# The last pair of a GNN kernel by batch element, its scores added on VectorE

## The chip, the cores and the metric

The kernel runs on one core of one Trainium2 chip. The metric is device time in microseconds of one execution. A core has TensorE (PE in the profile; its weight loads are PEld), VectorE (DVE), ScalarE (ACT), GpSimd (POOL) and SyncE (SP), each with its own instruction queue, and 16 DMA engines that all queues share.

## The reference

Two layers on 64 graphs of 256 nodes with 256 features; an adjacency matrix of zeros and ones for each graph. Each layer is `x = x + layer(relu(layernorm(x)))`. The first is a gated graph network of three steps, the second a graph attention with four heads:

```python
# layer 0, three steps
m = einsum('bnd,de->bne', h, weight[i])
aggr = einsum('bst,bsd->btd', A, m)
h = gru_cell(aggr, h, w_ih, w_hh, b_ih, b_hh)
# layer 1
h = (x @ W.T + b).reshape(B, N, H, C)
l_src, l_dst = einsum(h, a_src), einsum(h, a_dst)          # one score per node and head
logits = leaky_relu(l_src[:, :, None, :] + l_dst[:, None, :, :], 0.2)
logits = where(adj[..., None] == 1, logits, NEG_INF)
out = einsum('bijh,bjhc->bihc', softmax(logits, axis=2), h)
```

## The kernel before

Two batch elements make a pair; there are 32 pairs, numbered 0 to 31. All work is entered into a plan by tick and is emitted in that order (`at`, L307; L777 to 780). Pair p starts at tick 18p, so three pairs are under way at a time: while one runs its last step (its ticks 24 to 29), the one before it prepares its attention and the one before that computes its outputs. A tick has three phases, STEP, READY and REST, in this order, and within a phase the later pair comes first. Each engine carries out its instructions in the order in which they were emitted. Below, ticks of pair 31 are counted from its own start, and those of pair 30 are converted to that count (its own minus 18).

A step (`Step`, L365) has six ticks. It works on both elements together and shares products between them, so that its blocks of eight matmuls (`block`, L289; `pd`, `pc`, `pe`, `pn` are their PSUM banks) belong to both. `new_n` ends with a subtraction on GpSimd (L487), and `update` (L499) gives the new state of one element with two VectorE instructions. After the last step (`back`, L544) the state is transposed and added to x.

The attention of a pair then goes as follows; the ticks in brackets are those of pair 31 in the kernel before.

- `plan_norm` and `plan_relu_T` (32 to 36): statistics and normal form of the four row blocks of x on VectorE, one power on GpSimd, eight transposes and a Relu on ScalarE into `hT_b`.
- `bar` (35): VectorE makes the mask `noedge` from the integers `adj`, loaded by SP at tick 22.
- `values` (37, 38): products with the weights, `val`, and the scores of both kinds.
- `score_rows` (37, 38 for the two elements of the last pair): the scores are transposed, copied into `flat` (one buffer), and written to DRAM by SP. SP then reads the target scores back on all partitions, as `drow`.
- `linked` and `barred_in` (36 to 41): the mask is transposed (`plink`, `link`; one `link` buffer), and ScalarE fills the logits `zz` with it. `zz` has four buffers, two for each pair.
- `add_rows` (41, 42): GpSimd issues a DMA that adds the source scores from DRAM into `zz`.
- `maxima` (43 to 50) and `leaky` (48 to 55): the largest target score of each node among its neighbours, on VectorE; leaky relu, on ScalarE.
- `shift` and `shift_rows` (47 and 51 for the two elements): the row maxima, written to DRAM as `topT`. In the last pair SP reads them back as `mrow`, and VectorE adds them to `zz` in `exps`; in the other pairs a second adding DMA does it (pair 30: ticks 38 and 39).
- `exps` (60 to 63) and `output` (62 to 65): exponentials on ScalarE, 16 matmuls `po` for each of the four row blocks, division on VectorE, addition to x on GpSimd. At tick 66 SP writes out the pair.

Pair 30's maxima stand at ticks 25 to 32, its leaky relus at 30 to 37, its exponentials at 42 to 45, its outputs at 44 to 47. Pair 29's outputs stand at 26 to 29.

The lines that hold the order:

```python
STEP, READY, REST = range(3)
plan.setdefault(tick, ([], [], []))[phase].append((-p, fn))
...
for tick in sorted(plan):
    for phase in plan[tick]:
        for _, fn in sorted(phase, key=lambda y: y[0]):
            fn()
```

Of the kernel before, what the change touches and what calls it, by code (L numbers as in the profile page):

```python
# [9 lines left out]
F32 = mybir.dt.float32  # L10
# [16 lines left out]
def gated_gnn_then_gat_kernel(  # L27
# [282 lines left out]
    def plan_norm(src, name, p, ticks):  # L310

        v = {}

        def stats(r0):
            def fn():
                if not v:
                    v["st"] = small.tile([P, R, 6], F32, tag="st", name=f"st_{name}")
                    v["mv"] = small.tile([P, R, 2], F32, tag="mv", name=f"mv_{name}")
                for r in (r0, r0 + 1):
                    nc.vector.bn_stats(v["st"][:, r, :], src()[:, r, :])  # L320
                    nc.vector.bn_aggr(v["mv"][:, r, :], v["st"][:, r, :])
            return fn

        def deviation():
            rstd = v["rstd"] = small.tile([P, R], F32, tag="rstd", name=f"rstd_{name}")
            nc.vector.tensor_scalar_add(rstd, v["mv"][:, :, 1], EPS)
            nc.gpsimd.tensor_tensor(rstd, rstd, mhalf, ALU.pow)

        def result():
            xn = v["xn"] = buf("xn", [P, R, D], f"xn_{name}")  # L330
            for r in range(R):
                nc.vector.tensor_scalar(
                    xn[:, r, :], src()[:, r, :], v["mv"][:, r, 0:1], v["rstd"][:, r : r + 1],
                    op0=ALU.subtract, op1=ALU.mult,
                )

        for t, fn in zip(ticks, (stats(0), stats(2), deviation, result)):
            at(t, READY, p, fn)
        return v

    def plan_relu_T(v, tag, name, p, ticks):

        w = {}

        def fn(k):
            def go():
                if not w:
                    w["hT"] = buf(tag, [P, KD, T], f"hT_{name}")
                pt = bank(f"pt_{name}_{k}")
                for r in range(R):  # L350
                    nc.tensor.transpose(pt[:, ts(r, P)], v["xn"][:, r, ts(k, P)], ident)  # L351
                nc.scalar.activation(w["hT"][:, k, :], pt, AF.Relu)
            return go

        for k, t in enumerate(ticks):
            at(t, REST, p, fn(k))
        return w

    def by_c(y):
        return y.rearrange("q (c n) -> q c n", c=KD)  # L360

    def of(y, i):
        return y[:, :, ts(i, N)]

    class Step:  # L365


        def __init__(self, n_, l, hT):
            self.n_, self.l, self.hT = n_, l, hT

        def own(self, tag, shape):
            y = buf(tag, shape, f"{tag}_{self.n_}")
# [107 lines left out]
        def new_n(self, i):  # L480
            n__ = of(self.hn, i)
            p_n = by_c(getattr(self, f"pn{i}"))
            for c in range(KD):
                nc.scalar.activation(  # L484
                    n__[:, c, :], p_n[:, c, :], AF.Tanh, bias=bi[:, 2 * KD + c : 2 * KD + c + 1]
                )
            nc.gpsimd.tensor_sub(of(self.R, i), of(self.hT(), i), n__)  # L487

        def tick_5(self):
            self.first_n(1)  # L490
# [13 lines left out]

    def plan_pair(p):
        t0 = APART * p
        v = {}

        def ready(t, fn):
            at(t0 + t, READY, p, fn)  # L510
# [4 lines left out]
        def rest(t, fn):  # L515
            at(t0 + t, REST, p, fn)
# [27 lines left out]
        def back(l, i):  # L544

            def fn():
                if l < L - 1 and i == 0:
                    v["hN"] = node_halves(f"{p}_{l}")
                pt = bank(f"pback_{p}_{l}_{i}")
                for s in range(KN):  # L550
                    for k in range(KD):
                        nc.tensor.transpose(  # L552
                            pt[:, s * D + k * P : s * D + (k + 1) * P], h["hT"][:, k, ts(i * KN + s, P)], ident
                        )
                hi, lo, xi = (flat(y[:, i * KN : (i + 1) * KN, :]) for y in (*v["hN"], v["x"]))
                if l < L - 1:
                    nc.scalar.copy(hi, pt)  # L557
                    nc.vector.tensor_sub(lo, pt, hi)  # L558
                else:
                    nc.vector.tensor_add(xi, pt, xi)  # L560
            return fn

        for l in range(L):
            g = Step(f"{p}_{l}", l, lambda: h["hT"])
            t = 2 * SUB * l
            ready(t - 3 if l else t - 1, g.state_sums)
            ready(t + 2, g.last_state_sum)
            step(t, lambda g=g: g.tick_0(v["hN"], v["edge"]))
            for k, fn in enumerate((g.tick_1, g.tick_2, g.tick_3, g.tick_4, g.tick_5), 1):
                step(t + k, fn)  # L570
            ready(t + SUB, lambda g=g: g.update(0))
            ready(t + SUB, lambda g=g: g.update(1))
            for i in range(PB):
                rest(t + SUB + 1 + i, back(l, i))


        def load_adj_1():
# [5 lines left out]
            nc.vector.tensor_scalar(v["noedge"], v["adj"], 1.0, 16 * MASKED, op0=ALU.not_equal, op1=ALU.mult)  # L583

        rest(22, load_adj_1)
        xn_b = plan_norm(lambda: v["x"], f"b{p}", p, [t0 + 32, t0 + 33, t0 + 33, t0 + 34])
        ready(35, bar)
        hb = plan_relu_T(xn_b, "hT_b", f"b{p}", p, [t0 + 35, t0 + 36])

        last = p == NPAIR - 1  # L590
        units = [range(i, i + 1) for i in range(PB)] if last else [range(PB)]
        blocks_of = {u: slice(u.start * KN, u.stop * KN) for u in units}

        def values(r0):
            def fn():
# [12 lines left out]
                nc.vector.tensor_copy(v["score"][:, r0 : r0 + 2, :], v["val"][:, r0 : r0 + 2, S0:])  # L608
            return fn

        rest(37, values(0))
        rest(38, values(2))

        def as_rows(src, n, what, u):

# [13 lines left out]
            src = rows[h0 : h0 + H, :]  # L629
            return bass.AP(tensor=src.tensor, offset=src.offset, ap=[[0, P], [0, blocks], [1, H * N]])  # L630

        scores, tops, drow, mrow, logits, link = {}, {}, {}, {}, {}, {}

        def score_rows(u):
            def fn():
                scores.update(as_rows(v["score"][:, blocks_of[u], :], 2 * H, "score", u))
                for i in u:
                    drow[i] = buf("row", [P, H, N], f"drow_{p}_{i}")
                    nc.sync.dma_start(drow[i].rearrange("q h n -> q (h n)"), on_all(scores[i], H, 1)[:, 0, :])
            return fn  # L640

        for u in units:
            rest(39 + u.start if not last else 37 + u.start, score_rows(u))

# [24 lines left out]
                )  # L671
            return fn

        rest(36, linked(0))
        rest(39, linked(1))
        ready(38, barred_in(0, 0))
        ready(39, barred_in(0, 1))
        ready(40, barred_in(1, 0))
        ready(41, barred_in(1, 1))
        rest(41 if last else 43, add_rows(0, scores))  # L680
        rest(42 if last else 44, add_rows(1, scores))

        def maxima(r, h0):
            def fn():
# [35 lines left out]
                    )  # L720
            return fn

        for r in range(R):
            for y in range(H // 2):
                ready(43 + 2 * r + y, maxima(r, 2 * y))
                ready(48 + 2 * r + y, leaky(r, 2 * y))
        for u in units:
            t = 47 if last and u.start == 0 else 51
            ready(t, shift(u))
            rest(t + (0 if last else 1), shift_rows(u))  # L730
        if not last:
            rest(56, add_rows(0, tops))
            rest(57, add_rows(1, tops))

# [8 lines left out]
        def output(r):  # L743
            def fn():
                i, s = divmod(r, KN)
                po = bank(f"po_{p}_{r}")
                for h_ in range(H):
                    for j in range(KN):
                        nc.tensor.matmul(  # L749
                            po[:, ts(h_, VC)], logits[i][:, j, h_, ts(s, P)], v["val"][:, i * KN + j, ts(h_, VC)],  # L750
                            start=(j == 0), stop=(j == KN - 1),
                        )
                heads = po[:, :S0].rearrange("q (h c) -> q h c", h=H)
                rden = small.tile([P, H], F32, tag="rden", name=f"rden_{p}_{r}")
                nc.vector.reciprocal(rden, heads[:, :, C])
                o = buf("o", [P, D], f"o_{p}_{r}")
                nc.vector.tensor_mul(  # L757
                    o.rearrange("q (h c) -> q h c", h=H),
                    heads[:, :, :C],
                    rden[:, :, None].to_broadcast([P, H, C]),  # L760
                )
                nc.gpsimd.tensor_add(v["x"][:, r, :], v["x"][:, r, :], o)  # L762
            return fn

        for t, (i, j) in zip((60, 61, 62, 63), ((0, 0), (0, 1), (1, 0), (1, 1))):
            ready(t, exps(i, j))
        for r, t in enumerate((62, 63, 64, 65)):
            rest(t, output(r))
        rest(66, lambda: nc.sync.dma_start(out_rows[ts(p, T), :].rearrange("(r q) d -> q r d", q=P), v["x"]))


    at(SUB, REST, 0, lambda: step_weights(1))
# [38 lines left out]
```

## Time and profile before

| | us |
|---|---|
| three runs | 2613.26, 2613.37, 2610.36 |
| median | 2613.26 |
| profiled execution | 2612.2 |
| its span, first to last instruction | 2610.4 |
| busy in the span: PE / PEld / DVE / ACT / POOL | 2539.7 / 2266.0 / 1849.2 / 1462.2 / 653.0 |
| last matmul of pair 31's last step ends, about | 2533.9 |
| last attention product ends, about | 2604.6 |

The page divides the span into 40 slices of 65 us; a digit is a tenth. Lines of the chain and of the timeline begin with the start in the span and the length, both in microseconds; what stands in brackets is the engine's idle time before the instruction and what ended it. Lines of windows give the stretch, its length, the busy time of each engine with the number of its instructions, the clock granted to TensorE (1.00 is full), the share of the DMA engines and what they moved.

### The profile page before, as it was taken

To read this page: it belongs to the slowest core of one execution; us is meant where nothing else is said; L and a number is where in the kernel's file an instruction comes from. 1 tells how busy PE (TensorE), PEld (TensorE's weight loads), DVE (VectorE), ACT (ScalarE), POOL (GpSimd) and SP (SyncE) were. 2 spreads that over 40 slices of the span, in tenths; PEclk is the share of its full clock that TensorE was granted. 3 is DMA by queue.
4 is the path that set the end of the run, shared out by engine and by line. 5 is a ranking of instruction groups with operands and counts; after the bars stand their busy time and mean duration, and the time that the engine had idled before them with its cause. 6 is when DMAs were issued, how large, how long until landed. Compare 5 with 4: busy or idle time off the path is not lost.

```text
span 2610.4 us, 38818 instructions
## 1 busy us (share of the span) xinstructions
PE 2539.7 (97%) x14074; PEld 2266.0 (87%) x14074; DVE 1849.2 (71%) x4528; ACT 1462.2 (56%) x3077; POOL 653.0 (25%) x518
## 2 busy tenths in 40 slices
PE   6899999999999999999999999999999999999985
PEld 5688898888988888989888989888898888898975
DVE  4567777777776777777777777777777677777663
ACT  2346555655655665655665555565565566565553
POOL 0012222222223222222222322222222322222221
PEclk9899999999999999999999999999999999999995
DMA  3004344434344434344443334443434453433444
GB/s 89 19 9 94 89 110 98 110 85 90 82 106 98 114 84 88 92 95 106 106 98 92 84 88 110 98 111 85 90 81 106 98 114 84 89 92 86 98 98 114
DMA packets 120320, 239.89 MB, mean 92 GB/s; under 512 B 9792, under 2 KB 79424, under 8 KB 120128
## 3 DMA queue, kind: packets, MB, share of 16 engines
q0 software_dynamic: 34272, 132.13, 26.5%
q1 hardware_dynamic: 80160, 102.52, 12.9%
q10 hardware_dynamic: 5696, 2.76, 0.4%
q8 instruction: 111, 1.82, 0.3%
q14 instruction: 81, 0.66, 0.1%
HBM read 219.82 MB, written 17.56 MB: 91 GB/s over the span
## 4 chain that ended last, share of the span: by engine, by line
PE 95%; DVE 2%; DMA 1%; issue 1%; ACT 0%; POOL 0%; ACTq 0%; POOLq 0%; SPq 0%; DVEq 0%
PE pd L293 19%; PE pn L293 13%; PE pc L293 13%; PE po L749 9%; PE pa L418 7%; PE qb L396 6%; PE pe L293 6%; PE p L293 6%; PE qa L396 5%; PE pv L601 4%; PE pback L552 3%; PE pt_a L351 1%; PE pt_b L351 1%; PE plink L652 1%; PE pc L220 0%
## 5 line engine op out<-in xcount | busy, mean ns | idle before, releaser
L487 POOL TENSOR_TENSOR R<-hT_a,hn 128x512 f32<-128x512 f32 x192 | 318.3, 1658 | 883.7 <-ACT hn L484 840.9
L293 PE MATMUL pn<-aggr,w_a 128*128 128x256 f32 x1536 | 367.1, 382 | 0.0
L293 PE MATMUL pd<-T,w_a 128*128 128x256 f32 x1536 | 364.6, 380 | 0.0
L293 PEld LDWEIGHTS pn<-aggr,w_a 128*128 128x128 f32 x1536 | 287.1, 190 | 42.9 <-DVE pn L473 6.3
L293 PEld LDWEIGHTS pd<-T,w_a 128*128 128x128 f32 x1536 | 286.9, 190 | 36.9
L749 PEld LDWEIGHTS po<-val,zz 128*128 128x128 f32 x2048 | 258.7, 201 | 17.2 <-ACT zz L740 12.5
L749 PE MATMUL po<-val,zz 128*128 128x65 f32 x2048 | 255.9, 281 | 11.6 <-ACT zz L740 11.6
L689 DVE CUSTOM_DVE_ANT_0 any<-drow,noedge 128x256 f32<-128x256 f32 x512 | 244.7, 478 | 16.9 <-DMA drow<-score_dram 7.9
L762 POOL TENSOR_TENSOR x<-x,o 128x256 f32<-128x256 f32 x128 | 117.1, 915 | 498.2 <-DVE o L757 498.2
L484 ACT ACTIVATE hn<-pn,bi 128x256 f32<-128x256 f32 x384 | 160.4, 469 | 144.5 <-PE pn L293 144.4
L403 ACT ACTIVATE R<-pc,brz 128x256 f32<-128x256 f32 x192 | 80.5, 470 | 280.0 <-PE pc L293 280.0
L717 ACT ACTIVATE zz<-zz,val 128x256 f32<-128x256 f32 x512 | 231.7, 509 | 8.3 <-DMA zz<-score_dram 8.3
L502 DVE SCALAR_TENSOR_TENSOR R<-Z,R 128x512 f32<-128x512 f32 x192 | 131.8, 686 | 147.3 <-POOL R L487 142.7
L558 DVE TENSOR_TENSOR hNlo<-pback,hNhi 128x512 fp32r<-128x512 f32 x128 | 88.5, 691 | 196.2 <-ACT hNhi L557 196.2
L403 ACT ACTIVATE R<-pe,brz 128x256 f32<-128x256 f32 x192 | 80.5, 470 | 195.2 <-PE pe L293 195.2
L503 DVE SCALAR_TENSOR_TENSOR hT_a<-R,hn 128x512 f32<-128x512 f32 x192 | 175.0, 912 | 13.6 <-DVE R L502 0.5
L293 PE MATMUL pc<-hT_a,w_h 128*128 128x256 f32 x768 | 181.4, 379 | 0.0
L293 PE MATMUL pe<-aggr,w_a 128*128 128x256 f32 x768 | 181.4, 379 | 0.0
L293 PE MATMUL pc<-aggr,w_a 128*128 128x256 f32 x768 | 181.4, 379 | 0.0
L293 PE MATMUL pd<-T,w_h 128*128 128x256 f32 x768 | 181.4, 379 | 0.0
L293 PE MATMUL p<-T,w_a 128*128 128x256 f32 x768 | 181.4, 379 | 0.0
L473 DVE SCALAR_TENSOR_TENSOR pn<-R,hn 128x512 f32<-128x512 f32 x192 | 142.9, 744 | 52.0 <-ACT hn L399 27.4
(147 smaller groups left out, 5310.6 us busy)
## 6 DMA issues: line engine op xcount, KB each, us to landing
zz<-score_dram POOLq DMA_DIRECT2D x64, 1024.0 KB, 11.9
zz<-topT_dram POOLq DMA_DIRECT2D x62, 1024.0 KB, 8.1
adj<-in_adj_dram SPq DMA_DIRECT2D x64, 512.0 KB
drow<-score_dram SPq DMA_DIRECT2D x64, 512.0 KB
x<-in_x_dram SPq DMA_DIRECT2D x32, 512.0 KB
out_dram<-x SPq DMA_DIRECT2D x32, 512.0 KB
score_dram<-score SPq DMA_DIRECT2D x128, 4.0 KB
topT_dram<-topT SPq DMA_DIRECT2D x128, 2.0 KB
```

The source lines that it names most:

```text
L293: nc.tensor.matmul(pt[:, ts(c, N)], w[:, k, j * D + c * P : j * D + (c + 1) * P], src[:, k, :], start=start and c == 0 and k == 0, stop=(c ...
L396: nc.tensor.matmul(pt, w_n[:, j, :], src, start=start, stop=True, skip_group_check=True)
L403: nc.scalar.activation(of(dst, i)[:, c, :], src[:, c, :], AF.Tanh, bias=brz[:, g0 + c : g0 + c + 1], scale=0.5)
L418: nc.tensor.matmul(pt[:, ts(i, N)], hN[half][:, i * KN + s, ts(e, P)], edge[:, i * KN + s, :], start=(s == 0 and half == 0), stop=(s == KN ...
L473: nc.vector.scalar_tensor_tensor(by_c(self.bank(f"pn{i}")), of(self.R, i), 1.0, of(self.hn, i), op0=ALU.add, op1=ALU.mult)
L484: nc.scalar.activation(n__[:, c, :], p_n[:, c, :], AF.Tanh, bias=bi[:, 2 * KD + c : 2 * KD + c + 1])
L487: nc.gpsimd.tensor_sub(of(self.R, i), of(self.hT(), i), n__)
L502: nc.vector.scalar_tensor_tensor(d_, of(self.Z, i), 1.0, d_, op0=ALU.add, op1=ALU.mult)
L503: nc.vector.scalar_tensor_tensor(of(self.hT(), i), d_, 0.5, of(self.hn, i), op0=ALU.mult, op1=ALU.add)
L689: nc.vector.tensor_tensor_reduce(any_, drow[r // KN][:, h, :], v["noedge"][:, r, :], 1.0, -3.0e38, ALU.add, ALU.max, accum_out=v["top"][:, ...
L717: nc.scalar.activation(zz[:, h, :], zz[:, h, :], AF.Prelu, alpha=ALPHA, bias=v["val"][:, r, S0 + H + h : S0 + H + h + 1],)
L749: nc.tensor.matmul(po[:, ts(h_, VC)], logits[i][:, j, h_, ts(s, P)], v["val"][:, i * KN + j, ts(h_, VC)], start=(j == 0), stop=(j == KN - 1),)
```

## The change

It touches the last pair alone.

- Its last step subtracts on VectorE. `update(1)` goes from tick 30 to 31, the two `back` from 31 and 32 to 30 and 31.
- Normalisation, transposes and Relu go by element (`plan_norm_unit`): statistics at 31 and 33, normal form and transposes at 32 and 34. Values go to 33 and 35, the scores' rows to 34 and 36.
- The mask goes from tick 35 to 26, its transposes from 36 and 39 to 27 and 29, the fillings from 38 to 41 to 28 to 31.
- The source scores are loaded by SP on all partitions as plain rows (`trow`) and added on VectorE (`own_scores`, four additions of 128x1024); the two adding DMAs go.
- By element, at ticks 38 and 40 and the two after each: own scores, maxima, shift and its rows, leaky relu.
- Exponentials and outputs stand at ticks 43 and 44, the output's addition to x is VectorE's, and each element is stored on its own.

```diff
-        def __init__(self, n_, l, hT):
+        def __init__(self, n_, l, hT, hurry):
+            self.minus = nc.vector if hurry else nc.gpsimd
...
-            nc.gpsimd.tensor_sub(of(self.R, i), of(self.hT(), i), n__)
+            self.minus.tensor_sub(of(self.R, i), of(self.hT(), i), n__)
...
+            late = last and l == L - 1
+            ready(t + SUB + late, lambda g=g: g.update(1))
             for i in range(PB):
-                rest(t + SUB + 1 + i, back(l, i))
+                rest(t + SUB + (not late) + i, back(l, i))
...
+        if last:
+            hb = {}
+            for i in range(PB):
+                plan_norm_unit(lambda: v["x"], hb, f"b{p}", i, p, [t0 + 31 + 2 * i, t0 + 32 + 2 * i])
...
+        ready(26 if last else 35, bar)
...
+        rest(33 if last else 37, values(0))
+        rest(35 if last else 38, values(2))
...
                 for i in u:
+                    if last:
+                        trow[i] = buf("row", [P, H, N], f"trow_{p}_{i}")
+                        nc.sync.dma_start(trow[i].rearrange("q h n -> q (h n)"), on_all(scores[i], 0, 1)[:, 0, :])
                     drow[i] = buf("row", [P, H, N], f"drow_{p}_{i}")
...
+            rest(34 + 2 * u.start if last else 39, score_rows(u))
...
+        def own_scores(i):
+            def fn():
+                for j in range(KN):
+                    nc.vector.tensor_add(logits[i][:, j, :, :], logits[i][:, j, :, :], trow[i])
+            return fn
+        t = 28 if last else 38
+        rest(t - 2 + last, linked(0))
+        rest(t + 1, linked(1))
+        ready(t, barred_in(0, 0))
+        ready(t + 1, barred_in(0, 1))
+        ready(t + 2, barred_in(1, 0))
+        ready(t + 3, barred_in(1, 1))
...
+        if last:
+            for u in units:
+                t = 38 + 2 * u.start
+                ready(t, own_scores(u.start))
+                for r in range(u.start * KN, u.stop * KN):
+                    for y in range(H // 2):
+                        ready(t + 1, maxima(r, 2 * y))
+                        ready(t + 2, leaky(r, 2 * y))
+                ready(t + 1, shift(u))
+                rest(t + 1, shift_rows(u))
...
-                nc.gpsimd.tensor_add(v["x"][:, r, :], v["x"][:, r, :], o)
+                (nc.vector if last else nc.gpsimd).tensor_add(v["x"][:, r, :], v["x"][:, r, :], o)
+                if last and s == KN - 1:
+                    write(i * KN, KN)
...
+        for t, (i, j) in zip((43, 43, 44, 44) if last else (60, 61, 62, 63), ((0, 0), (0, 1), (1, 0), (1, 1))):
             ready(t, exps(i, j))
+        for t, r in zip((43, 43, 44, 44) if last else (62, 63, 64, 65), range(R)):
             rest(t, output(r))
```

`plan_norm_unit` for an element i at its two ticks:

```python
# first tick, READY: bn_stats and bn_aggr of two row blocks, rstd + EPS on VectorE, pow on GpSimd
# second tick, READY: two tensor_scalar into xn
# second tick, REST: four transposes into one bank, one Relu on ScalarE into the element's part of hT_b
```

More of the change, by code (lines that the diff above doesn't have):

```diff
@@ L357, in plan_relu_T, with plan_norm_unit, stats, result @@
         return w
+    def plan_norm_unit(src, w, name, i, p, ticks):
+        v = {}
+        rows = slice(i * KN, (i + 1) * KN)
+        def stats():
+            v["mv"] = small.tile([P, KN, 2], F32, tag="mv", name=f"mv_{name}_{i}")
+            st = small.tile([P, KN, 6], F32, tag="st", name=f"st_{name}_{i}")
+            for s in range(KN):
+                nc.vector.bn_stats(st[:, s, :], src()[:, i * KN + s, :])
+                nc.vector.bn_aggr(v["mv"][:, s, :], st[:, s, :])
+            rstd = v["rstd"] = small.tile([P, KN], F32, tag="rstd", name=f"rstd_{name}_{i}")
+            nc.vector.tensor_scalar_add(rstd, v["mv"][:, :, 1], EPS)
+            nc.gpsimd.tensor_tensor(rstd, rstd, mhalf[:, :KN], ALU.pow)
+        def result():
+            if i == 0:
+                w["xn"] = buf("xn", [P, R, D], f"xn_{name}")
+                w["hT"] = buf("hT_b", [P, KD, T], f"hT_{name}")
+            for s, xn in enumerate(w["xn"][:, r, :] for r in range(rows.start, rows.stop)):
+                nc.vector.tensor_scalar(
+                    xn, src()[:, i * KN + s, :], v["mv"][:, s, 0:1], v["rstd"][:, s : s + 1],
+                    op0=ALU.subtract, op1=ALU.mult,
+                )
+        def turned():
+            pt = bank(f"pt_{name}_{i}")
+            for k in range(KD):
+                for s in range(KN):
+                    nc.tensor.transpose(
+                        pt[:, k * N + s * P : k * N + (s + 1) * P], w["xn"][:, i * KN + s, ts(k, P)], ident
+                    )
+            nc.scalar.activation(of(w["hT"], i), by_c(pt), AF.Relu)
+        at(ticks[0], READY, p, stats)
+        at(ticks[1], READY, p, result)
+        at(ticks[1], REST, p, turned)
     def by_c(y):
@@ L506, in plan_pair @@
         t0 = APART * p
+        last = p == NPAIR - 1
         v = {}
@@ L563, in plan_pair @@
         for l in range(L):
-            g = Step(f"{p}_{l}", l, lambda: h["hT"])
+            g = Step(f"{p}_{l}", l, lambda: h["hT"], last and l == L - 1)
             t = 2 * SUB * l
@@ L571, in plan_pair @@
             ready(t + SUB, lambda g=g: g.update(0))
-            ready(t + SUB, lambda g=g: g.update(1))
+            late = last and l == L - 1
+            ready(t + SUB + late, lambda g=g: g.update(1))
             for i in range(PB):
-                rest(t + SUB + 1 + i, back(l, i))
+                rest(t + SUB + (not late) + i, back(l, i))
         def load_adj_1():
@@ L585, in plan_pair @@
         rest(22, load_adj_1)
[L586 to L590, printed above, removed]
         units = [range(i, i + 1) for i in range(PB)] if last else [range(PB)]
         blocks_of = {u: slice(u.start * KN, u.stop * KN) for u in units}
+        if last:
+            hb = {}
+            for i in range(PB):
+                plan_norm_unit(lambda: v["x"], hb, f"b{p}", i, p, [t0 + 31 + 2 * i, t0 + 32 + 2 * i])
+        else:
+            xn_b = plan_norm(lambda: v["x"], f"b{p}", p, [t0 + 32, t0 + 33, t0 + 33, t0 + 34])
+            hb = plan_relu_T(xn_b, "hT_b", f"b{p}", p, [t0 + 35, t0 + 36])
+        ready(26 if last else 35, bar)
         def values(r0):
@@ L609, in values @@
             return fn
-        rest(37, values(0))
-        rest(38, values(2))
+        rest(33 if last else 37, values(0))
+        rest(35 if last else 38, values(2))
         def as_rows(src, n, what, u):
@@ L630, in on_all @@
             return bass.AP(tensor=src.tensor, offset=src.offset, ap=[[0, P], [0, blocks], [1, H * N]])
-        scores, tops, drow, mrow, logits, link = {}, {}, {}, {}, {}, {}
+        scores, tops, trow, drow, mrow, logits, link = {}, {}, {}, {}, {}, {}, {}
         def score_rows(u):
@@ L642, in plan_pair @@
         for u in units:
-            rest(39 + u.start if not last else 37 + u.start, score_rows(u))
+            rest(34 + 2 * u.start if last else 39, score_rows(u))
         def linked(i):
@@ L672, in add_rows @@
             return fn
[L674 to L681, printed above, removed]
+        def own_scores(i):
[10 more added lines that the diff above has]
+        ready(t + 3, barred_in(1, 1))
+        if not last:
+            rest(43, add_rows(0, scores))
+            rest(44, add_rows(1, scores))
         def maxima(r, h0):
@@ L721, in leaky @@
             return fn
[L723 to L731, printed above, removed]
+        if last:
[8 more added lines that the diff above has]
+                rest(t + 1, shift_rows(u))
+        else:
+            for r in range(R):
+                for y in range(H // 2):
+                    ready(43 + 2 * r + y, maxima(r, 2 * y))
+                    ready(48 + 2 * r + y, leaky(r, 2 * y))
+            ready(51, shift(units[0]))
+            rest(52, shift_rows(units[0]))
             rest(56, add_rows(0, tops))
@@ L761, in fn, with write @@
                 )
-                nc.gpsimd.tensor_add(v["x"][:, r, :], v["x"][:, r, :], o)
-            return fn
-        for t, (i, j) in zip((60, 61, 62, 63), ((0, 0), (0, 1), (1, 0), (1, 1))):
+                (nc.vector if last else nc.gpsimd).tensor_add(v["x"][:, r, :], v["x"][:, r, :], o)
+                if last and s == KN - 1:
+                    write(i * KN, KN)
+            return fn
+        def write(r0, n):
+            nc.sync.dma_start(
+                out_rows[p * T + r0 * P : p * T + (r0 + n) * P, :].rearrange("(r q) d -> q r d", q=P),
+                v["x"][:, r0 : r0 + n, :],
+            )
+        for t, (i, j) in zip((43, 43, 44, 44) if last else (60, 61, 62, 63), ((0, 0), (0, 1), (1, 0), (1, 1))):
             ready(t, exps(i, j))
-        for r, t in enumerate((62, 63, 64, 65)):
+        for t, r in zip((43, 43, 44, 44) if last else (62, 63, 64, 65), range(R)):
             rest(t, output(r))
-        rest(66, lambda: nc.sync.dma_start(out_rows[ts(p, T), :].rearrange("(r q) d -> q r d", q=P), v["x"]))
+        if not last:
+            rest(66, lambda: write(0, R))
     at(SUB, REST, 0, lambda: step_weights(1))
```

## The prediction

> **What bounds the kernel now.** I read the page's busy row and clock row first, then windows of the tail, then the chain of waits and the timeline from 2500 us on, then the DMA view in half-microsecond windows.
>
> ```profile
> PE 2539.7 (97%) x14074; PEld 2266.0 (87%) x14074; DVE 1849.2 (71%) x4528; ACT 1462.2 (56%) x3077; POOL 653.0 (25%) x518
> PEclk9899999999999999999999999999999999999995
> ```
>
> TensorE is busy 97% of the span at full clock. Only the last of the 40 clock digits is 5, so all that an edit to the last pair alone can win lies in some 75 us at the end. Windows (us, busy PE, PEld, DVE, ACT, POOL, then clock, DMA share, GB/s):
>
> ```profile
> 2534.00:2536.00 2.00, 1.60 (x15) 1.46 (x14) 0.26 (x2) 2.00 (x6) 1.18 (x1) 1.00 0.00 0
> 2538.00:2540.00 2.00, 1.46 (x6) 1.12 (x7) 1.86 (x6) 1.53 (x4) 0.00 (x0) 0.50 0.73 257
> 2568.00:2570.00 2.00, 2.00 (x11) 2.00 (x11) 1.86 (x11) 0.00 (x0) 0.99 (x1) 0.50 1.09 221
> ...
> 2596.00:2600.00 4.00, 4.00 (x21) 4.00 (x20) 0.82 (x3) 1.06 (x1) 1.52 (x2) 0.50 0.00 0
> ```
>
> The step ends near 2536 at full clock. Afterwards TensorE mostly waits, and the attention products `po` (L749) run at half clock however busy they are. The chain of waits (start, length) says what the tail consists of:
>
> ```profile
> 2533.87 1.75 PE po L749 x16
> ...
> 2554.32 6.93 DMA score_dram<-score
> ...
> 2565.96 10.09 PE po L749 x46
> ...
> 2579.04 3.33 PE po L749 x16
> ...
> 2591.09 10.09 PE po L749 x46
> ```
>
> One `po` costs 1.75 us at full clock and, by the spacing of its reciprocals in the timeline (2597.79, 2601.20, 2604.61), 3.41 us at half. Pair 30's four `po` stand at 2565 to 2582.4, under pair 31's own preparation; pair 31's four run from 2590 to 2604.6. The end is 5.8 us after the last `po` (division, POOL add, 512 KB store).
>
> The mask load that the change uses earlier, in the timeline, and its queue's last packets (DMA view, window 2524.5 to 2525.0; the next half microsecond has none):
>
> ```profile
> 2511.94 0.42 SPq L114 DMA_DIRECT2D adj<-in_adj_dram  x1
> 2519.61 0.70 DVE L457 TENSOR_TENSOR pe<-pd,m 128x512 f32<-128x512 f32 x1 [0.68 <-PE pd L293]
> 2548.56 0.67 DVE L583 TENSOR_SCALAR noedge<-adj 128x1024 bf16<-128x1024 int32 x1
> ```
>
> ```profile
> q1 hardware_dynamic: 2, 0.00, 0.9%
> ```
>
> Nothing else is on q1 then, so `adj` has landed at about 2525.0, 13 us after issue: it is behind two `drow` and shares the engines with two 1 MB accumulations. Its use at 2548.56 never showed it.
>
> **What the Trainium skill says.** "DMA: Bandwidth & Descriptors", Queues, rings and completion order: the engines take turns between queues and a transfer is complete only when every engine has reported. The trace agrees: most of `adj` moved by 2519, a trickle lasted to 2525. "TensorE: Matmul & The Clock Gate", Part 1: an idle window of about 3.4 us halves the clock, a busy one restores it. The fall agrees (half by 2538, two microseconds after the last matmul); the recovery does not for `po`, which stayed at 0.50 through 10 and 13 us of unbroken work. The same page, on queue depths: ScalarE and VectorE are strictly first in, first out. Agrees: the `link` copy at 2561.57 sat behind a score copy that waited 5.21 us, although its matmuls had ended at 2556.7.
>
> **The change part by part.**
>
> (1) *Mask in the last step.* `bar` goes to tick 26, just behind the T4n subtraction that ended at 2517.5. It must wait for `adj`: 2525.0, plus 0.67 = 2525.7. Queued behind it on VectorE: two maxima (0.9), a `po` division (0.6), then `pe` (L457, 0.6), which therefore ends at 2527.9, not 2520.2. On TensorE the four `plink` transposes now follow block pc, done at 2521.2, and need `bar`: they run at 2525.7 (0.25), then the `po` 1.75, qb 0.5, and block pd with RZ, which also needs `pe` to have read its bank, at 2528.2. Before, it started at 2523.45: **+4.8**. TensorE is idle 4.5 us in it. The window in which the clock fell near 2537.6 was about 43% busy, and an idle stretch of 4.5 us leaves some window less busy, so I expect half clock until a fully busy window has passed: some 5 us at half speed, **+2.5** (bounds 0 and 3.4).
>
> (2) *Fillings.* Four `zz<-link` of 1.04 us on ScalarE, two link copies (0.42), eight transposes (0.45) move from the tail into ticks 27 to 31. The first `zz` fits into ScalarE's gaps. The second stands after the step's last tanh, and since there is one `link` buffer the second link copy waits for it: 1.05 us later than that tanh, and ahead of the last `po` division and update(0) on VectorE. The subtraction L487 moves from POOL (1.27) to VectorE (about 0.65, as the 128x512 TENSOR_TENSOR L384): POOL was not the last to release (division at 2535.64), so nothing is won, and the maxima behind it come later. Together **+1.2** (0 to 2).
>
> So update(0) ends at U = 2538.1 + 4.8 + 2.5 + 1.2 = **2546.6**.
>
> (3) *By element from U.* Back and x add 1.9 (a maximum pair between), update(1) 1.4, stats 1.3, POOL pow 1.25 (hides the next x add partly), result 1.2, transposes and relu 1.6, values 3.0 (2.3 to 3.6 in the trace), val and score 0.8, result of element 1 and its transposes 1.6 (they precede the scores on both engines), score transpose and copy 0.7: SP issues at U + 14.7. Before it was 2554.0 - 2538.1 = 15.9: only 1.2 gained.
>
> (4) *Plain rows.* Removed: two SW accumulations of 1 MB, the first issued at 2561.79 and used at 2573.33 (11.5 us). Added: two `trow` loads on SP and four VectorE adds of 1.22 (as L739). The score write sees an idle DMA, because pair 30's `topT` is now queued behind it on SP: 1.6 us (as `topT` at 2579.39) in place of 7.2. `trow` lands 4.2 us after issue (as `drow` at 2511.06): U + 20.5. VectorE gets there at U + 22, held by the single `flat` buffer until pair 30's `topT` has been written. Adds 2.5, eight maxima 3.75, shift, transpose, copy 1.4: U + 29.6. Then `topT` write and `mrow` load: 1.6 + 3.8 alone, up to 5.5 + 5 now that pair 30's 2 MB of accumulation runs at the same time (issued near U + 20, 10.6 us each). Adds and exp 3.6: first `po` of pair 31 at **T = U + 40 to 44**, about 2588.5. SP's queue per element: two score writes (0.6), the wait for them, two row loads (0.35 each), and later two `topT` writes (0.6), a wait, `mrow` (0.35) and a store (0.4). Pair 30's four `topT` writes wait behind the first of these, and so do its accumulations on POOL and its exps on ScalarE. One of those exps stands ahead of pair 31's, but its data lands near U + 31, before T: no cost.
>
> (5) *Order of the products.* Pair 31's outputs stand at ticks 43, 43, 44, 44; pair 30's at 44 to 47, and within a tick the later pair comes first. So all four of pair 30 stand behind all four of pair 31 on TensorE's queue, and the cover at 2565 to 2582 is gone: eight `po` in a row, 8 x 3.41 = 27.3. Between the second and third, VectorE reaches element 1's `mrow` adds only after output(1): 1.0 + 2 x 1.22 + 1.05 + 0.2 = 4.7 idle. The last output is pair 30's, by POOL, and its 512 KB: 5.8 as before. Pair 31's adds moved to VectorE (0.42) and its split store lie under this and cost nothing.
>
> Sum: 2588.5 + 27.3 + 4.7 + 5.8 = 2626.3 against a span of 2610.4: **+15.9**. The profiled run took 2612.2 (1.8 around the span), 1.1 under the median of the three; I put the difference on the median: 2613.3 + 15 (rounded down for the upper bounds taken in 1) = **2628**.
>
> **Rivals.**
> A: the mask arrives in time (no wait at tick 26). For it: 13 us of landing depends on other transfers' luck. Against: last packet at 2524.5 to 2525, 7 us late, and nothing ahead of it changes. U = 2539.3, T = 2581.3, end 2619.1: +8.7, **2622**.
> B: full clock for the eight `po`: 14 in place of 27.3, a price of 13.4. For it: the skill's rule. Against: both stretches at 0.50. It decides towards faster from T of 2581 or less (T + 13.9 + 4.7 + 5.8 below 2605.2), thus with A or with lighter DMA: **2604 to 2608**. With the wait of (1) it gives +2.5: **2616**, no change.
> C: pair 30's accumulations and the single `flat` buffer cost as much per element as in the slow case twice, or the clock stays half to the end of the step: +8 more, **2636**.
> That the change isn't what it says: scores, mask and fillings are moved as told, but the scores' adds themselves can only run after the step, which (4) has.
>
> **How the numbers follow.** Forecast 60%, A 15%, B faster 10%, B no change 10%, C 5%. A measurement of this kernel can tell about 0.2%, 5.2 us, from none. Slower 0.80, same 0.10, faster 0.10. The range 2611 to 2637 leaves out B's fast end and the end of C.
>
> **What would show it.** Right: `noedge` (L583) waits about 7 us on DMA near 2518 and `pe` follows it at 2527; TensorE idles 4 us before `plink`, the clock dips there; eight `po` at about 3.4 us end the program, pair 30's last; a gap near 4.7 after the second. Wrong: `noedge` without a wait, `po` at 1.75, or pair 31's first `po` before 2575.

## The result and the profile after

The changed kernel is slower. Four runs took 2631.68 to 2639.30 us, median 2636.23, against 2612.61 of the kernel before beside them: ratio 1.0090, 95% interval 1.0073 to 1.0108. The profiled execution took 2639.3 us, its span is 2637.5.

The page's busy row and clock row of the changed kernel:

```profile
PE 2545.4 (97%) x14074; PEld 2269.7 (86%) x14074; DVE 1854.7 (70%) x4539; ACT 1462.4 (55%) x3077; POOL 644.0 (24%) x511
PEclk8899999999999999999999999999999999999975
```

TensorE does the same 14074 matmuls; the row now ends in 7 and 5, where it ended in 9 and 5. The mask's instruction in the timeline, and the chain of waits around it (start, length):

```profile
2529.44 0.69 DVE L625 TENSOR_SCALAR noedge<-adj 128x1024 bf16<-128x1024 int32 x1 [11.96 <-DMA adj<-in_adj_dram]
```

```profile
2511.97 17.44 DMA adj<-in_adj_dram
2529.44 0.70 DVE noedge L625
...
2530.80 3.42 PE po L815 x16
...
2535.18 3.25 PE pd L293 x8
2538.42 1.73 PE pe L293 x8
```

VectorE stood 11.96 us for `adj`. The transposes `plink` came only then, the product `po` behind them took 3.42 us and the block `pd` 3.25, and `pe` is the first at its old 1.73. The windows show the clock beside it (stretch, length, busy PE, PEld, DVE, ACT, POOL, then clock, DMA share, GB/s):

```profile
2520.00:2524.00 4.00, 0.00 (x0) 0.00 (x0) 0.00 (x0) 1.44 (x3) 0.00 (x0) 1.00 1.08 223
2524.00:2530.00 6.00, 0.00 (x0) 0.00 (x0) 0.56 (x1) 0.00 (x0) 0.00 (x0) 0.54 0.81 162
2530.00:2538.00 8.00, 7.81 (x30) 7.00 (x31) 4.61 (x16) 0.47 (x1) 1.44 (x2) 0.50 0.01 2
2538.00:2546.00 8.00, 8.00 (x46) 7.28 (x45) 3.37 (x9) 3.98 (x9) 1.10 (x1) 0.99 0.00 0
...
2611.00:2631.00 20.00, 19.99 (x94) 20.00 (x94) 3.89 (x12) 1.85 (x2) 2.17 (x3) 0.50 0.04 14
```

TensorE is idle for ten microseconds in the middle of the step, its clock falls to half at about 2524.5, and the next 8 us of work run at half. The last window is the end of the program: 20 us of unbroken products at half clock. The chain through the tail:

```profile
2582.30 10.04 DMA topT_dram<-topT
2592.40 3.80 DMA mrow<-topT_dram
...
2599.80 6.67 PE po L815 x30
...
2611.01 16.92 PE po L815 x78
```

A write of two pieces of 2 KB (`topT`) took 10 us. The run of products began at 2599.8, and there is a gap of 4.5 us behind the second. All eight stand in one row, pair 30's at the end.

### The profile page after: what moved, and what is told of

Read it like the earlier page. It is cut to its first block, busy times and chain, and to the rows that moved or that the text cites. A ratio compares the mean times of both kernels' runs of the same rounds, so it can differ in the third digit from the quotient of the medians.

```text
span 2637.5 us, 38812 instructions
## 1 busy us (share of the span) xinstructions
PE 2545.4 (97%) x14074; PEld 2269.7 (86%) x14074; DVE 1854.7 (70%) x4539; ACT 1462.4 (55%) x3077; POOL 644.0 (24%) x511
## 4 chain that ended last, share of the span: by engine, by line
PE 94%; DVE 2%; DMA 2%; issue 1%; ACT 0%; SPq 0%; POOL 0%; ACTq 0%; POOLq 0%; DVEq 0%
PE pd L293 19%; PE pn L293 13%; PE pc L293 12%; PE po L815 9%; PE pa L458 7%; PE qb L436 6%; PE pe L293 6%; PE p L293 6%; PE qa L436 5%; PE pv L647 4%; PE pback L593 3%; PE pt_a L351 1%; PE pt_b L351 1%; DMA adj<-in_adj_dram 1%; PE plink L701 1%
## 5 line engine op out<-in xcount | busy, mean ns | idle before, releaser
L815 PEld LDWEIGHTS po<-val,zz 128*128 128x128 f32 x2048 | 260.1, 202 | 13.2 <-ACT zz L806 8.6
```

Of the source, the lines that this page charges most:

```text
L815: nc.tensor.matmul(po[:, ts(h_, VC)], logits[i][:, j, h_, ts(s, P)], v["val"][:, i * KN + j, ts(h_, VC)], start=(j == 0), stop=(j == KN - 1),)
```

## The experiments

Each ratio is to the kernel before, run on the same chip beside it (its medians there: 2610.15 for e1 to e4, 2612.37 for e5 to e8, 2612.51 for e9 to e12). The changed kernel's is 1.0090.

| run | edit | median us | ratio, 95% interval |
|---|---|---|---|
| e1_adj_early | mask's load earlier | 2625.75 | 1.0054 (1.0039 to 1.0069) |
| e2_pair30_first | pair 30's products first | 2624.54 | 1.0054 (1.0039 to 1.0069) |
| e3_adds_late | pair 30's adding transfers later | 2629.57 | 1.0070 (1.0055 to 1.0085) |
| e4_mask_after_step | mask and its fillings of `zz` out of the step | 2624.80 | 1.0051 (1.0034 to 1.0068) |
| e5_filler | too many filler matmuls | 2634.71 | 1.0081 (1.0064 to 1.0097) |
| e6_early_and_first | e1 and e2 | 2615.73 | 1.0015 (1.0008 to 1.0021) |
| e7_no_adds | no adding transfers, products in a row | 2604.87 | 0.9973 (0.9964 to 0.9983) |
| e8_rows_alone | before, with plain rows alone | 2613.66 | 1.0005 (0.9996 to 1.0014) |
| e9_order_clock | e7, other order, fillers | 2597.13 | 0.9940 (0.9923 to 0.9956) |
| e10_after_clock | changed kernel, right fillers | 2624.97 | 1.0047 (1.0032 to 1.0062) |
| e11_before_clock | before, fillers | 2614.49 | 1.0008 (0.9999 to 1.0016) |
| e12_order_only | e9 without fillers | 2608.34 | 0.9985 (0.9978 to 0.9991) |

### The wait for the mask: e1 and e4

```diff
-        rest(22, load_adj_1)
+        rest(12 if p == NPAIR - 1 else 22, load_adj_1)
```

> The changed kernel, but the last pair's adjacency is loaded at its tick 12 instead of 22; nothing else moves. Theory W (the wait for adj at tick 26 is paid in full, because VectorE and TensorE are in order and everything after follows from it): noedge no longer waits (it waited 11.96 us in the changed kernel's profile), no fall of the clock in the step, update(0) of pair 31 ends near 2540 instead of 2552.2, and the whole run is 10 to 13 us shorter, about 2625 us. Rival H (the tail waits on transfers that start late anyway, so a late step is absorbed): 0 to 3 us shorter. In neither case is it faster than the kernel before (2612.6), because the eight products in a row remain.

```diff
-        ready(26 if last else 35, bar)
+        ready(32 if last else 35, bar)
-        t = 28 if last else 38
+        t = 34 if last else 38      # linked at 33 and 35
```

> The changed kernel, but mask, its transposes and fillings go out of the last step again: the mask at tick 32, transposes at 33 and 35, fillings at 34 to 37. Undoes this one part of the change. Theory W: the wait is gone, as with the early load, and the moved work costs 0 to 3 us of it in the tail: 8 to 13 us shorter, 2624 to 2628. Rival (the fillings in the step are worth their wait, because they block the scores in the tail): less than 5 us shorter. The difference to the early load measures what moving the fillings into the step is worth by itself once the wait is gone.

Both are 10.5 and 11.4 us shorter by their medians, 9 to 10 by the ratios. The timeline with the early load:

```profile
2518.51 0.68 DVE L625 TENSOR_SCALAR noedge<-adj 128x1024 bf16<-128x1024 int32 x1
...
2538.73 1.10 DVE L543 SCALAR_TENSOR_TENSOR hT_a<-R,hn 128x512 f32<-128x512 f32 x1
```

No bracket: the mask waits for nothing. The first element's new state ends at 2539.8, not at 2552.2, 12.4 us earlier, and the span of this profiled execution is 13.2 us shorter (2624.3 against 2637.5): the wait was not absorbed. With mask and fillings out of the step the times overlap with those of e1 (2622.56 to 2625.03 against 2624.01 to 2626.58), so moving the fillings into the step is worth nothing that these runs show, even when nothing waits for it.

### The order of the products: e2, and both repairs: e6

```diff
-  (43, 43, 44, 44) if last ...  exps
-  (43, 43, 44, 44) if last ...  output
+  (46, 46, 47, 47) if last ...  exps
+  (48, 48, 49, 49) if last ...  output
```

> The changed kernel, but pair 31's exponentials go to ticks 46, 46, 47, 47 and its outputs to 48, 48, 49, 49, so that pair 30's four outputs (ticks 44 to 47) come first on TensorE. Theory O (the order cost: pair 30's four products stood behind a wait for pair 31's exponentials although their own logits were ready earlier): pair 30's products start near 2593, right behind its exponentials, pair 31's follow without a gap at about 2606.6, the stall of 4.5 us between the second and third product goes, and the run is 9 to 12 us shorter, about 2626. Rival (pair 30's logits are not ready before pair 31's either, since its own adding transfers land as late): under 5 us shorter.

> The changed kernel with both single repairs: the last pair's adjacency loaded at tick 12, and pair 31's exponentials and outputs behind pair 30's. Alone they were worth 10.5 and 11.7 us. If the two costs stand one after the other on the same path, they add: about 2614, within 3 us of the kernel before (2610.2), because what is left of the change's gain (lighter transfers, shorter preparation) pays for eight products in a row less little. If they hide each other: 2620 or more.

The timeline of e2 shows all eight products as one entry:

```profile
2596.54 27.47 PE L815 MATMUL po<-val,zz 128*128 128x65 f32 x128
```

It begins 3.5 us later than expected: 1.4 us because the mask came later in this profile (2530.8), the rest because pair 31's second `topT` transpose, at 2596.37, stands ahead of it on TensorE. It has no gap, and the run is 11.7 us shorter by the median, 9.4 by the ratio. With both repairs the gains add up, within 2 us: 20.5 us together by the medians, 10.5 and 11.7 alone; 19.6 together by the ratios, 9.4 and 9.4 alone. What is left of the change is then 1.0015, still a little slower than before. The wait and the order are most of its loss, and the rest, as it stands, brings no gain; what the last 0.15% consists of was not taken apart.

### The traffic in the tail: e3 and e8

```diff
+  # pair 30's two add_rows(tops) are issued in pair 31's tick 42, behind
+  nc.gpsimd.tensor_add(g, mrow[1][:, 0, :4], mrow[1][:, 0, :4])
+  # exps of pair 30: own ticks 62, 62, 63, 63
```

> The changed kernel, but pair 30's two adding transfers of the row maxima (1 MB each) are issued by GpSimd only after pair 31's second mrow has landed (a small addition that reads mrow stands in front of them), and pair 30's exponentials two ticks later accordingly. Theory C (contention: pair 31's topT write took 10.0 us and its second trow load 10 us because those transfers run at the same time): the topT write takes under 2.5 us, trow under 5, pair 31's first product starts 6 to 8 us earlier (near 2591 on the same scale), and pair 30's additions still land under pair 31's products; 5 to 8 us shorter, about 2630. Rival (small writes are slow in the tail whatever else runs): topT stays over 6 us and the time within 3 us.

SyncE's queue in e3:

```profile
2575.82 0.60 SPq L672 DMA_DIRECT2D topT_dram<-topT  x2
2577.37 0.34 SPq L770 DMA_DIRECT2D mrow<-topT_dram  x1
```

The reading back could be issued 1.55 us after the write, not 10.4 us as in the changed kernel (2582.00 to 2592.40). In those 1.5 us the DMA engines were busy to a share of 0.01; in the changed kernel, from 2582 to 2590, all the time. From the first element's new state to the first product it is 39.1 us (2546.2 to 2585.4), not 46.4. The run is 6.7 us shorter by the median, 5.2 by the ratio. So the 10 us of the small write came from the two adding transfers, either directly or through pair 31's own rows, which ran beside both in the changed kernel and had landed before the write in e3.

The other half, plain rows in the kernel before:

```diff
+  trow[i] loaded by SP in score_rows, own_scores(0) at tick 42, own_scores(1) at 46
-  rest(41 if last ..., add_rows(0, scores)); rest(42 if last ..., add_rows(1, scores))
```

> The kernel before with one part of the change alone: the last pair's source scores come as plain rows and are added by VectorE (ticks 42 and 46) in place of the two adding DMAs. If the adding transfers set pair 31's time in the kernel before: 3 to 8 us shorter (2602 to 2607). If VectorE's own queue does (its maxima stand between the divisions of pair 30's products, and its adds are 4.9 us more): within 3 us of 2610.2, or up to 4 us longer.

1.0005: nothing. The timeline shows why the rows brought no gain. The score write still stood beside pair 30's adding transfers and took 7.2 us (2551.7 to 2558.9), against 7.3 in the kernel before. The leaky relus could start 5.7 us earlier, counted from the first element's new state; but VectorE, with 4.9 us more to do, came to the `mrow` additions at 2586.3, and counted in the same way that is 50.5 us, against 49.5 in the kernel before:

```profile
2564.07 2.36 DVE L686 TENSOR_TENSOR zz<-zz,trow 128x1024 f32<-128x1024 f32 x2 [4.50 <-DMA trow<-score_dram]
2586.32 2.34 DVE L752 TENSOR_TENSOR zz<-zz,mrow 128x1024 f32<-128x1024 f32 x2
```

### The clock of the products: e5, e10, e11

```diff
+  for _ in range(n):
+      nc.tensor.matmul(pt[:, :N], w_n[:, 0, :], w_h[:, 0, :N], start=True, stop=True)
```

> The changed kernel with matmuls that compute nothing needed (128x256 float32 into a free bank, 40 behind pair 31's first topT transpose, 12 behind the second, 14 between its second and third attention product), so that TensorE enters the eight products at full clock. Settles rival B of the prediction. If the products' half clock is only a matter of how cold TensorE is when they begin: they run at 1.75 us each in place of 3.41 from the first to the last, and the run is 10 to 14 us shorter (about 2623). If the products by themselves don't count as work enough (they stayed at 0.50 for 10 and 13 us in the kernel before): full clock for the first one or two, half within 3 to 7 us, and 0 to 4 us shorter, or up to 3 longer.

> The changed kernel with the same idea as the run with fillers, but as many as the gaps hold: a float32 filler is two passes, so the 66 of that run took twice the time meant and pushed pair 31's first product from 9 us behind its second topT transpose's cover. Here 22 behind pair 31's first topT transpose, 7 behind the second, 9 between its second and third product. Theory (once at full clock the products keep it): eight at 1.78 us in place of 3.41, 10 to 14 us shorter than the changed kernel: 2622 to 2627, still slower than before because of the wait for the mask. Rival (the earlier run kept its clock only because of its many fillers): clock falls among the last six products, 4 to 8 us shorter.

> The kernel before with fillers alone (13 ahead of pair 30's products, 14 behind its third, 12 and 5 around pair 31's second topT transpose) and nothing of the change. If the half clock of the products costs there too: pair 31's four products at 1.78 in place of 3.41, of which its second element's wait for mrow (2593 in the profile) leaves about half: 3 to 5 us shorter, 2607 to 2610. If pair 31's exponentials bound the end: within 2 us of before.

A filler is a matmul whose result nobody reads; it only keeps TensorE busy. In e5 each filler shows as two matmuls, not one (x80 for 40), so the first 40 took 19.5 us and delayed the products by some 7 us (25.2 us from pair 31's first `topT` transpose to the first product, 18.5 in the changed kernel). But the chain of waits shows what clock the products had:

```profile
2583.55 19.53 PE filler L850 x80
...
2608.37 3.52 PE po L815 x32
...
2617.99 8.89 PE po L815 x80
```

Two products in 3.52 us, five in 8.89: 1.76 to 1.78 each, to the end. e10 has fillers that fit the gaps, and its windows (PE alone, then clock, DMA share, GB/s) say the same:

```profile
2596.00:2600.00 4.00, 4.00 (x35) 1.00 0.29 119
...
2605.00:2616.00 11.00, 10.71 (x94) 1.00 0.08 26
```

It is 11.3 us shorter than the changed kernel by the median. Part of that may be the mask, which waited 8.44 us in e10's profile and 11.96 in the changed kernel's; the products by themselves took 1.78 in place of 3.41. e11 is a miss: fillers alone do nothing for the kernel before. For one thing, the clock fell among its products:

```profile
2582.00:2591.00 9.00, 8.78 (x47) 1.00 0.36 120
2591.00:2598.00 7.00, 6.09 (x33) 0.67 0.23 75
2598.00:2606.00 8.00, 7.10 (x33) 0.50 0.00 0
```

It fell near 2593.3, after some 1.1 us of scattered idleness in 2.6 us; in e10 0.4 us was harmless, and in e9 0.7. Where the limit lies stays open. For another, these fillers delayed pair 31's first `topT` transpose, from 2578.7 to 2581.3; counted from the first element's new state that is 4.6 us, of which 3.2 reach pair 31's first product. The run doesn't separate the two.

### A version that beats both: e7, e12, e9

```diff
+  e4's mask and fillings; pair 30's row maxima read back as mrow and added by VectorE
+  pair 31's second element (own scores to leaky relu) one tick later
+  exps at pair 31's ticks: pair 30 40, 40, 41, 41; pair 31 43, 43, 44, 44
+  products: pair 30 40, 40, 41, 42; pair 31 43, 43, 44, 44; divisions later, on their own ticks
```

> A version meant to beat both. From the changed kernel: mask and fillings behind the last step (as in the run with the mask after the step), pair 30's row maxima also as plain rows added on VectorE (no adding transfers left in the tail), and the products in the order 30, 30, 30, 30, 31, 31, 31, 31, emitted apart from their divisions so that VectorE isn't held by them; pair 30's begin as soon as two of its blocks are exponentiated. Theory: the eight products run without a gap from about 2572, 27.3 us, and the end lies 4 to 6 us behind: 2603 to 2607, faster than the kernel before by 0.1 to 0.3%. Rival: VectorE, which gets 4.9 us more work and all additions in a row, is late for pair 31's second element and opens a gap of 3 to 8 us: 2608 to 2614.

```diff
+  e12: exps and products of pair 30's second element at 43, pair 31's from 44
+  e9: e12 and fillers (13 and 7 around the first topT transpose, 3 and 6 around the second)
```

> The version of the run with order and fillers, without the fillers: separates the two. At half clock eight products take 27.3 us from about 2571 on; the order moves no product's start unless VectorE had held it: 2603 to 2607, within 2 us of the version without adding transfers (2604.9). If the order is what helps, it is near the run with fillers instead, 2598 to 2602.

> The version without adding transfers, with two further edits: pair 30's second element is exponentiated and multiplied behind pair 31's maxima instead of ahead of them, so that pair 31's second element isn't held by them on VectorE; and matmuls that compute nothing needed fill TensorE's gaps (13 before and 7 behind the first topT transpose, 3 before and 6 behind the second), so that the eight products start at full clock, which the run with fillers showed they then keep (six in 10.83 us). Theory: products at 1.78 us, pair 31's last ends near 2591 to 2593 on a scale where the step's last update ends near 2537, and the whole is 2598 to 2601 us, 4 to 7 under the version without adding transfers (2604.9). Rival: VectorE's order bounds the end and the clock is won in vain: 2602 or more.

e7 is 0.27% faster than before. Its products stand in a row:

```profile
2571.36 10.07 PE po L820 x46
2581.43 0.21 PE ptopT L666
2581.65 17.23 PE po L820 x80
```

e12 was expected within 2 us of it and is 3.5 slower. Pair 30's third product now waits behind pair 31's maxima: TensorE stands 2.65 us for its exponential and starts it at 2579.0; the other products follow without a gap, so the delay reaches the end. Whether this order is the better one at full clock no run shows, since none has e7's order with fillers. What the fillers are worth in e12's order is shown: e9 is 11.2 us shorter than e12, and 0.60% (0.44 to 0.77) faster than the kernel before:

```profile
2573.64 3.52 PE po L820 x32
...
2582.34 10.72 PE po L820 x94
```

## Why the prediction was right, and where its sizes were off

The forecast was slower, 2628 in a range of 2611 to 2637. The median is 2636.23: direction and mechanism came as forecast, but the range held by 0.8 us only, and two of the four runs lie above it, so that it held at all is partly luck. The profiled execution is 27.1 us longer, the median 23.6, where the sum said 15.9. The steps against the changed kernel's trace:

| step | predicted | measured |
|---|---|---|
| (1) `adj` has landed | 2525.0 | 2529.4 |
| (1) TensorE idle in the step | 4.5 | 10.6 |
| (1) half clock in the step costs | 2.5 (0 to 3.4) | about 4.0 |
| (1), (2) first element's state, U | 2546.6 | 2552.2 |
| (4) score write | 1.6 | 1.6 |
| (4) first `topT` issued, from U | 29.6 | 29.8 |
| (4) `topT` write | 1.6 to 5.5 | 10.0 |
| (4) `mrow` load | 3.8 to 5 | 3.8 |
| (4) first product, T - U | 40 to 44 | 46.4 |
| (5) one product; gap behind the second | 3.41; 4.7 | 3.41; 4.5 |
| (5) from the last product to the end | 5.8 | about 6.1 |

Of the 11.2 us between the sum and the profile, 5.6 lie before U, 4.5 between U and T, and about 1.0 behind T.

**(1) was right in kind.** VectorE waited, `pe` and the transposes waited behind it, TensorE's clock fell. Removing the wait (e1, e4) gave 9 to 11 us. Its size was off mostly in one term: the landing of `adj` was read from one execution as if it were fixed. It is not: from the load's issue to the start of `noedge` it took 17.5 us in this profile (2511.97 to 2529.44), and 13.2, 17.0, 14.1 and 15.6 in those of e3, e2, e10 and e5; the kernel before's packets, on which the prediction rested, ended 13 after the issue. The spread of the runs fits this: 7.6 us for the changed kernel and 7.8 to 8.3 for e2, e3 and e5, which keep the wait, but 2.5 to 2.7 for e1, e4 and e6, which don't. It isn't proof: e10 keeps the wait, and its four runs spread over 2.0. The half clock cost 4.0, more than the upper bound of 3.4: `plink`, `po`, `qb` and `pd` took 8.2 us, against 4.2 by the full-clock durations that the prediction had. The Trainium skill, "TensorE: Matmul & The Clock Gate", Part 1, has the fall after an idle window of about 3.4 us, and this trace agrees: the clock fell 4.9 us after the last matmul. The fall in the kernel before, which the prediction called an agreement, is not one. It came near 2537.3 (the window from 2537.0 to 2537.5 has a mean of 0.76), not 2537.6, so 1.6 us after the last matmul; the stretch of 3.4 us that ends there (an estimate, with the window that the page states) was about half busy, not 43%.

**(2) was half right.** The second link copy never waited for the one `link` buffer. In e1 it follows VectorE's maxima at 2537.07, when ScalarE had been done with the buffer for half a microsecond. The step's end comes about 0.6 later, counted from the end of its last `po` (3.1 us to U, 2.5 in the kernel before). In e4, without any link copy there, it comes as late: the subtraction on VectorE, with two maxima behind it, is enough for that.

**(3)** held: SP issued the scores at U + 15.0, for 14.7.

**(4)** failed in one term, the write of `topT`. Up to its issue the sum held to 0.2 us. The prediction saw that pair 30's two adding transfers would run beside the write, but bounded it at 5.5, although it had itself read 7.2 us for a score write beside such transfers; it took 10.0, beside pair 31's own rows too. e3, which moves those transfers away, brings it under 1.6. What the prediction called no cost, pair 30's exponential ahead of pair 31's, was none: it started at 2590.85, before T. The Trainium skill, "DMA: Bandwidth & Descriptors", Queues, rings and completion order, lets the engines take turns between queues, a packet at a time, which would make a small write wait between the packets of large transfers; that this is how it was held up no run shows apart.

**(5)** held to a few tenths, and e2 shows the order to be worth 9 to 12 us.

**Rivals.** A didn't happen in any profile that kept the load at tick 22 and the mask at 26: the mask waited 7.8 to 12.3 us in all five. B is refuted for the changed kernel, since its products stayed at 0.50 for 20 us. But the prediction had the products run at half clock "however busy they are", and that is too wide: e5 and e10 show that they keep full clock once they have it. They only fail to raise it. The Trainium skill, "TensorE: Matmul & The Clock Gate", Part 1, says that a busy window restores the clock: 20 us of busy TensorE in the changed kernel did not, and the measurement decides. C named 2636, the measured number, but only one of its causes is there, in part: pair 30's adding transfers cost 4.5 us more than bounded, on the path to the first product. The clock was full again before the step ended (`pe` at 1.73), and the late landing of `adj`, 4.4 us of the excess, C doesn't name. Its number is a coincidence.

## What to carry to other kernels

Before a load is used earlier, find its last packet, not its issue, and take it from several executions; then look at what stands behind the waiting instruction on its engine and on TensorE. Where work is reordered by ticks, look at which finished work now stands behind a wait in the same queue: here four products that had filled a gap. In a tail at half clock, filling TensorE's gaps with idle matmuls can win more than moving work (e9 against e12: 11.2 us). The fillers must not delay what the products wait for, as in e5 and e11, and little idleness may be left among the products (0.7 us in e9, while 1.1 us cost e11 its clock).

## What the runs showed of the hardware

- Products of 128x65 float32 with a weight load each didn't raise the clock from half in 20 us of unbroken work (the changed kernel), and kept it full for 10.7 us once it was full (e10).
- Filler matmuls of 128x256 float32 raised it within about 4 us (e10: begun at 2577.7 at half clock; the window from 2580 to 2585 has a mean of 0.85, so the rise was near 2581.5).
- A write of two pieces of 2 KB to DRAM was over 1.0 us after its last issue with the DMA engines otherwise idle (e3, share 0.01), and 9.8 us after it beside two adding transfers of 1 MB and two loads of 512 KB (the changed kernel). A 512 KB load beside such transfers was usable 13 to 17.5 us after its issue.
